# Eight-layer network, top-two experts: tiles stepped by their own age, and one buffer pool opened earlier

## Chip, core and metric

One NeuronCore of a Trainium2 chip runs the whole program in one launch. The metric is device time in microseconds (us); lower is better. Each time is that of one execution, and the median of three executions stands for a kernel.

## The reference

A post-norm stack over x of 4 batch elements, 1024 positions and 128 features: eight sublayers, each followed by `x = layernorm(x + f(x))`. In order: a minGRU, a slot mixer, sparse attention, a two-way routed FFN, a linear "cosformer" attention, a top-two-of-eight expert FFN, a state-space layer (SSM) and a top-p expert FFN. The change is in the sixth, and touches its neighbours, the fifth (called *attention* below) and the seventh (called the *scan*):

```python
def _L2_ffn_ref(x, router_w, w13, w2):          # E, H, I, K = 8, 128, 256, 2
    logits = jnp.einsum('bsh,eh->bse', x, router_w)
    probs = jax.nn.softmax(logits, axis=-1)
    weights, indices = jax.lax.top_k(probs, K)
    weights = weights / (weights.sum(axis=-1, keepdims=True) + 1e-06)
    h13 = jnp.einsum('bsh,ehi->bsei', x, w13)
    gate, up = jnp.split(h13, 2, axis=-1)
    y = jnp.einsum('bsei,eih->bseh', jax.nn.silu(gate) * up, w2)
    y_sel = jnp.take_along_axis(y, indices[..., None], axis=2)
    return (y_sel * weights[..., None]).sum(axis=2)

# of the state-space layer, the step that makes the scan:
h = jnp.exp(d_l[:, :, None] * A) * h + (d_l * x_l)[:, :, None] * b_l[:, None, :]
y_l = jnp.einsum('ben,bn->be', h, c_l)
```

## The kernel before, in words

The program is written with a tile framework. Buffers come from named pools; a pool takes the place of pools closed before it, and what is written into it waits until whatever used that place is done. A planner then orders each engine's instructions by simulated times and priorities; only the TensorE order inside attention is kept as the code writes it (`manual_schedule`). Engines run their queues in order: PE (matmul), DVE (vector), ACT (activation), POOL (GpSimd), and SP, which issues most DMAs.

**Generators as the clock.** Sublayers are Python generators that other loops advance, one `next` at a time. The attention `l2_attn` runs 128 units (4 elements x 4 quarters x 8 head pairs) in steps `t` from -2; each step emits parts of several units and then advances the side generators. In the trace a step takes about 5.9 us.

**Sorting (`l2_dispatch`, one element at a time).** After an element's last attention quarter is normed, its 1024 rows are routed (`router`, L1209 on), counted and placed on DVE with small tiles of the pool `moed` (the variable `md`), and then scattered by 16 indirect DMAs on POOL (L1383) into a DRAM table `xrows` of 23 tiles of 128 rows, sorted by expert. When the scatters are emitted, the element's entry gets `"put"`. For the last element, attention stops its sorting before the scatters and leaves the rest to the scan's loop (`m2["rest"]`).

**Top-two experts (`l2_ffn`, the generator `moe`).** It has 92 units, 4 elements x 23 tiles. A unit goes through five stages: `l2_load_rows` (four tiles of sorted rows, SP, L1442), `l2_weights` (the tile's expert weights, tile `wx`, SP, L1458; 4 buffers), `l2_load_tile` (transposes), `l2_hidden` (eight matmul records into `pa_m` or `ph`, then ACT Tanh L1490 and DVE L1491 and L1494), `l2_expert_out` (four matmul records, ACT copy L1510, and for each fourth tile a store to `yrows`, L1512). In the loop before, one counter `t` places them: rows at unit `t+8`, weights at `t+4`, transposes at `t+2`, hidden at `t`, output at `t-2`. At the top of a step a `while` holds the counter as long as unit `t+8` belongs to an element whose rows have not been put. So when the next element isn't sorted yet, the current element's last tiles are held too: those with weights not yet loaded, not yet hidden, not yet put out. After an element's last tile comes `l2_combine` as a side generator: two halves, each of 8 indirect gathers on POOL (L1529), ACT scaling, DVE adds and a layernorm, some 12 `yield`s a half. It is advanced twice a step, and once a step while the counter is held.

**Who advances `moe`.** In attention, `early` advances it once a step after element 0 has been put and until element 1 is done. When element 0 is done (`st[0]["done"]`), attention also starts `begin`, the preparation of the scan's first half (`l3_prepare`), one part a step. In the scan loop (`l3`), there are 8 halves (element x half of the positions), each of 16 state steps `n`; `moe` is advanced once per `n`, twice in the first half, and `rest` once per `n`.

**The scan (`l3_scan`).** Each `n` loads two rows broadcast over partitions (`bn`, `cn`, SP, L1844), multiplies on POOL (`db`, L1849), takes the exponent on ACT (`da`, L1853), scans on DVE (L1854), multiplies again on POOL (`hc`, L1865), and sums on PE (`pys`). The top-p experts (`l3_ffn`, `ph` and `py`) of finished halves are interleaved, and the last two halves' experts run after the last scan.

**Where the pools lie.** Pools stack from two sides, left and right. On the right, from the end inward: `moek`, `first`, `moet` (the experts' tiles), `w2` (attention's weights: `wE`, `c_turn` and so on), and innermost `moed`. On the left, attention's `cos` is closed when attention ends, and the scan's pools `ssm` (`sq3`, `xc`, `db1` ...) and `ssm2` (`bn`, `cn`, `db`, `hc`, `xnT`, `ud` ...) take its place and more. In the bytes of a partition that the planner gave them: `cos` 59,424 to 126,752, `ssm` 59,424 to 78,144, `ssm2` 78,144 to 156,280, `moed` 150,336 to 159,744 (9,408 long), `w2` 159,744 to 189,504 (29,760 long). `moed` and `w2` are closed together, when attention's code ends; `top` (the top-p experts' tiles) takes their place.

Of the kernel before, what the change touches and what calls it, by code (L numbers as in the profile page):

```python
# [37 lines left out]
NT2 = 2 * T // P + NE - 1  # L38
# [11 lines left out]
def weave(*gens):  # L50

    gens = list(gens)
    while gens:
        for g in gens[:]:
            if next(g, gens) is gens:
                gens.remove(g)


class Net:
# [1342 lines left out]
    def l2_ffn(self, wp):  # L1402

        units = [
            dict(st=st, j=j, n=min(4, NT2 - j // 4 * 4))
            for st in self.m2["st"]
            for j in range(NT2)
        ]  # L1410
        n = len(units)
        side = []
        for t in range(-8, n + 4):
            while t + 8 < n and "put" not in units[max(t + 8, 0)]["st"]:
                for g in side[:]:
                    if next(g, self) is self:
                        side.remove(g)
                yield
            if 0 <= t + 8 < n and units[t + 8]["j"] % 4 == 0:
                self.l2_load_rows(units[t + 8], units, t + 8, wp)  # L1420
            if 0 <= t + 4 < n:
                self.l2_weights(units[t + 4], wp)
            if 0 <= t + 2 < n:
                self.l2_load_tile(units[t + 2], units, t + 2, wp)
            if 0 <= t < n:
                self.l2_hidden(units[t], wp)
            if 0 <= t - 2 < n:
                u = units[t - 2]
                self.l2_expert_out(u, units, t - 2, wp)
                if u["j"] == NT2 - 1:  # L1430
                    side.append(self.l2_combine(u["st"], wp))
            for g in side * 2:
                if next(g, self) is self and g in side:
                    side.remove(g)
            yield
        for g in side:
            yield from g

    def l2_load_rows(self, u, units, i, wp):
        j, n, st = u["j"], u["n"], u["st"]  # L1440
# [720 lines left out]
def program(tc, io):  # L2161
    with ExitStack() as ctx:
        n = Net(ctx, tc, io)
        wd, w0 = ExitStack(), ExitStack()
        wdp = wd.enter_context(tc.tile_pool(name="wd", bufs=1))
        W = n.l0_load(w0.enter_context(tc.tile_pool(name="w0", bufs=1)))
        d = n.l1_ffn_load(wdp)
        dp = ctx.enter_context(
            tc.tile_pool(name="rows", bufs=2, space=bass.MemoryType.DRAM)
        )  # L2170
        sd = ctx.enter_context(tc.tile_pool(name="ssmd", bufs=2, space=bass.MemoryType.DRAM))
        with ExitStack() as ff:
            last = n.front(ff, w0, W, d, dp)
            keep = ctx.enter_context(tc.tile_pool(name="moek", bufs=1, side="right"))
            first = ctx.enter_context(tc.tile_pool(name="first", bufs=1, side="right"))
            mt = ctx.enter_context(tc.tile_pool(name="moet", bufs=2, side="right"))
            w2 = ExitStack()
            n.l2_attn_load(w2.enter_context(tc.tile_pool(name="w2", bufs=1, side="right")))
            weave(*last)
        wd.close()  # L2180
        def load():
            n.l2_ffn_load()
            n.l3_load(sd)
            n.l2_rows(keep, md, dp)

        moe = n.l2_ffn(mt)
        with w2:
            md = w2.enter_context(tc.tile_pool(name="moed", bufs=1, side="right"))
            n.l2_attn(load, n.l2_dispatch, moe, first)
        n.l3_pools(ctx)  # L2190
        fp = ctx.enter_context(tc.tile_pool(name="top", bufs=2, side="right"))
        n.l3(moe, fp)
# [17 lines left out]
```

## Time and profile before

| what | value |
|---|---|
| three executions | 2287.27, 2295.73, 2288.26 us; median 2288.26 |
| the profiled execution | 2286.79 us, of it 2285.0 in the span from first to last instruction |
| mean granted TensorE clock | 0.935 |
| busy: PE, DVE, ACT, POOL | 1978.9, 1349.2, 1210.5, 1023.4 us |
| indirect scatters (L1383) of elements 0 to 3, first to last | 840 to 915, 1007 to 1094, 1216 to 1305, 1371 to 1393 us |
| gathers (L1529) of elements 0 to 3, first to last | 1169 to 1200, 1361 to 1410, 1544 to 1582, 1724 to 1772 us |
| first `db` multiply of the scan's halves 0 to 7 | 1390, 1476, 1563, 1668, 1778, 1871, 1961, 2058 us |

How to read it: times inside the trace count from the start of the span. Attention lies between some 615 and 1340 us, the scan from 1390 to 2147, and from there to 2281 the last experts run on PE. A group row gives an engine, a line, what is written and read, the count, and busy time. A window row gives its length, then the busy time of each engine with its instruction count, the granted clock, and the DMA engines' share. In an answer in order of time, the columns are start, length, engine, line, operation and tiles, and in brackets how long the engine sat idle before it and what is taken to have released it.

### The profile page before, as it was taken

The numbers are of one execution on the slowest core, as the hardware profiler recorded it, in microseconds if no ns is written. First come the engines' busy times: TensorE is split into PE (matmuls) and PEld (weight loads), VectorE is DVE, ScalarE is ACT, GpSimd is POOL, SyncE is SP. The second block draws the span as 40 slices with busy tenths as digits, with TensorE's granted clock in tenths as the row PEclk, the third lists the DMA queues.
The fourth block names the chain that finished last, engine by engine and source line by source line (L and its number), as shares of the span: only waits on it lengthen the run. The fifth ranks groups of instructions, "written<-read, shape, count | busy, mean of one in ns | idle before, by whom it ended". The sixth has DMA issues, their size and how long they took to land.

```text
span 2285.0 us, 46402 instructions
## 1 busy us (share of the span) xinstructions
PE 1978.9 (87%) x17806; PEld 1383.3 (61%) x17806; DVE 1349.2 (59%) x3693; ACT 1210.5 (53%) x2623; POOL 1023.4 (45%) x812
## 2 busy tenths in 40 slices
PE   6667979879999999999989876679899999999998
PEld 3455655444477777787767664246565656565666
DVE  6457843433355565565555555696777688776521
ACT  6543443332244444444455456576768786767443
POOL 5100230000023234224233418998889889879400
PEclk9667989979999999999999988799999999999999
DMA  3000110005000010031223147456786677776421
GB/s 107 0 14 24 30 39 1 19 10 174 1 3 2 3 35 15 17 87 49 65 80 85 37 126 221 135 175 200 216 216 178 174 189 192 193 187 167 119 61 51
DMA packets 138559, 211.10 MB, mean 92 GB/s; under 512 B 18598, under 2 KB 75937, under 8 KB 137953
## 3 DMA queue, kind: packets, MB, share of 16 engines
q1 hardware_dynamic: 126192, 173.87, 25.5%
q0 software_dynamic: 12144, 34.26, 7.1%
q8 instruction: 140, 2.29, 0.4%
q14 instruction: 83, 0.67, 0.1%
HBM read 160.29 MB, written 23.16 MB: 80 GB/s over the span
## 4 chain that ended last, share of the span: by engine, by line
PE 43%; DVE 12%; ACT 11%; issue 3%; DMA 2%; POOL 1%; SPq 0%; ACTq 0%; DVEq 0%; POOLq 0%
PE py L127 7%; PE ph L127 7%; PE po L1126 5%; PE pqk L127 5%; PE pa_m L127 5%; DVE db L1854 4%; PE pys L127 3%; PE kp_mo L127 3%; PE pv L127 2%; PE pr L1196 2%; ACT hh L1980 1%; ACT da L1853 1%; PE pt L131 1%; PE kp_mo L131 1%; ACT xN L174 1%
## 5 line engine op out<-in xcount | busy, mean ns | idle before, releaser
L1059 POOL TENSOR_TENSOR qt<-r_q,sb_c_turn 128x256 f32<-128x256 f32 (+1 forms) x256 | 164.0, 660 | 447.9 <-ACT r_q L1051 442.2
L1865 POOL TENSOR_TENSOR hc<-db,cn 128x1024 f32<-128x1024 f32 x128 | 314.7, 2493 | 57.1 <-PE pys L127 25.6
L127 PEld LDWEIGHTS py<-wh,hh 128*128 128x128 f32 x2048 | 249.8, 192 | 79.9 <-issue 44.8
L1849 POOL TENSOR_TENSOR db<-ud,bn 128x1024 f32<-128x1024 f32 x112 | 286.3, 2633 | 12.4 <-issue 9.9
L127 PE MATMUL ph<-xT,wh 128*128 128x512 f32 x512 | 256.3, 618 | 21.2 <-DVE h_acc L1996 5.8
L127 PE MATMUL py<-wh,hh 128*128 128x128 f32 x2048 | 258.2, 276 | 12.7 <-ACT hh L1980 6.6
L1980 ACT ACTIVATE hh<-ph,sb_cols 128x512 f32<-128x512 f32 x256 | 170.6, 680 | 131.1 <-PE ph L127 104.5
L1117 DVE TENSOR_TENSOR a<-pa_m,sb_c_near 128x256 f32<-128x256 f32 x256 | 96.6, 419 | 203.4 <-PE pa_m L127 203.4
L1074 ACT ACTIVATE kN<-kp_mo,sb_c_trig 128x128 f32<-128x128 f32 x448 | 129.8, 371 | 132.0 <-PE kp_mo L131 122.2
L1853 ACT ACTIVATE da<-dl,aneg 128x512 f32<-128x512 f32 x224 | 153.6, 689 | 74.4 <-DVE db L1854 73.3
L127 PE MATMUL pys<-hc,sb_c_ident 128*128 128x512 f32 x324 | 158.5, 619 | 22.7 <-POOL hc L1865 19.4
L1854 DVE TENSOR_TENSOR_SCAN db<-da,carry,db 128x512 f32<-128x512 f32 x128 | 156.9, 1265 | 11.7 <-ACT da L1853 8.8
L1854 DVE TENSOR_TENSOR_SCAN db<-da,db 128x512 f32<-128x512 f32 x128 | 149.3, 1205 | 10.4 <-POOL db L1849 6.0
L127 PEld LDWEIGHTS ph<-xT,wh 128*128 128x128 f32 x512 | 89.6, 196 | 104.7 <-issue 53.5
L1996 DVE SCALAR_TENSOR_TENSOR h_acc<-py,gt,h_acc 128x128 f32<-128x128 f32 x256 | 71.9, 342 | 125.8 <-PE py L127 125.8
L127 PE MATMUL pqk<-xT,wE 128*128 128x256 f32 x512 | 136.7, 390 | 8.3 <-ACT coT L1193 4.2
L127 PEld LDWEIGHTS pys<-hc,sb_c_ident 128*128 128x128 f32 x324 | 60.5, 199 | 86.7 <-issue 58.7
L729 POOL DMA_INDIRECT orows<-o,ix x20 | 18.9, 944 | 186.0 <-DVE o L727 160.4
L127 PEld LDWEIGHTS pqk<-xT,wE 128*128 128x128 f32 x512 | 88.5, 193 | 21.9 <-DVE cv L1036 8.1
L131 PE MATMUL pt<-sb_c_ident,xN 128*128 128x128 f32 x224 | 54.2, 345 | 51.0 <-ACT xN L174 31.8
L1193 ACT COPY coT<-pt 128x512 f32<-128x512 f32 x64 | 37.5, 586 | 114.9 <-PE pt L131 114.9
L127 PE MATMUL po<-ht,wD 128*128 128x512 f32 x192 | 93.7, 595 | 0.0
(456 smaller groups left out, 4344.1 us busy)
## 6 DMA issues: line engine op xcount, KB each, us to landing
wx<-in_wF SPq DMA_DIRECT2D x92, 384.0 KB, 3.4
bn<-rows SPq DMA_DIRECT2D x128, 256.0 KB, 5.0
cn<-rows SPq DMA_DIRECT2D x128, 256.0 KB, 4.2
wh<-in_wH SPq DMA_DIRECT2D x64, 512.0 KB, 3.8
hc<-hc POOLq DMA_DIRECT2D x47, 512.0 KB, 6.6
xrows<-zero SPq DMA_DIRECT2D x4, 1472.0 KB, 12.3
xg<-xrows SPq DMA_DIRECT2D x20, 256.0 KB, 3.0
yrows<-ys SPq DMA_DIRECT2D x20, 256.0 KB, 3.3
```

The costliest lines, as they stand in the source:

```text
L127: return self.nc.tensor.matmul(out=out, lhsT=lhsT, rhs=rhs, start=start, stop=stop)
L131: self.nc.tensor.transpose(out, in_, self.ident[0:n, 0:n])
L1059: nc.gpsimd.tensor_mul(u["qt"][:, m, a:], u["q"][:, a:], c2["turn"][:, m, o + a : o + 2 * P])
L1074: self.nc.scalar.activation(u["kN"][:, c, m, :], pk[:, c, :], AF.Copy, scale=trig[:, k, m : m + 1])
L1117: nc.vector.tensor_mul(u["a"][:, i, :, :], pa[i], self.c2["near"][:, None, :].to_broadcast([P, 2, P]),)
L1126: self.nc.tensor.matmul(out=u["po"][self.HALF[j], i, c, :], lhsT=lhsT, rhs=rhs, start=key not in u["begun"], stop=True, skip_group_check=True,
L1849: nc.gpsimd.tensor_mul(db, ud, bc[0])
L1853: nc.scalar.activation(da, dl[:, ec, :], AF.Exp, scale=aneg[:, j : j + 1])
L1854: nc.vector.tensor_tensor_scan(db[:, ec, :], da, db[:, ec, :], carry[:, ec, n : n + 1] if h else 0.0, ALU.mult, ALU.add,)
L1865: nc.gpsimd.tensor_mul(hc, db, bc[1])
L1980: nc.scalar.activation(ht, ph, AF.Relu, bias=self.col("h_b1", i=e * NK + k))
L1996: nc.vector.scalar_tensor_tensor(acc[:, c, :], py[:, c, :], gt[:, c, e : e + 1], acc[:, c, :], ALU.mult, ALU.add,)
```

## The change

Two edits. In `l2_ffn` the one counter becomes an age per unit: a unit enters at age 0 when its element's rows are put, one per step, and does rows at age 0, weights at 4, transposes at 6, hidden at 8, output at 10, whether or not another unit follows; the side generators get two advances in every step. In `program` the pool `moed` is opened before `w2` instead of just before attention, so that from the end inward the right side is `moek`, `first`, `moet`, `moed`, `w2`. By the sizes above `moed` then has 180,096 to 189,504 and `w2` 150,336 to 180,096.

```diff
-        n = len(units)
-        side = []
-        for t in range(-8, n + 4):
-            while t + 8 < n and "put" not in units[max(t + 8, 0)]["st"]:
-                for g in side[:]:
-                    if next(g, self) is self:
-                        side.remove(g)
-                yield
-            if 0 <= t + 8 < n and units[t + 8]["j"] % 4 == 0:
-                self.l2_load_rows(units[t + 8], units, t + 8, wp)
-            if 0 <= t + 4 < n:
-                self.l2_weights(units[t + 4], wp)
-            if 0 <= t + 2 < n:
-                self.l2_load_tile(units[t + 2], units, t + 2, wp)
-            if 0 <= t < n:
-                self.l2_hidden(units[t], wp)
-            if 0 <= t - 2 < n:
-                u = units[t - 2]
-                self.l2_expert_out(u, units, t - 2, wp)
-                if u["j"] == NT2 - 1:
-                    side.append(self.l2_combine(u["st"], wp))
+        side, live, k = [], [], 0
+        stages = (
+            (0, lambda i: units[i]["j"] % 4 == 0 and self.l2_load_rows(units[i], units, i, wp)),
+            (4, lambda i: self.l2_weights(units[i], wp)),
+            (6, lambda i: self.l2_load_tile(units[i], units, i, wp)),
+            (8, lambda i: self.l2_hidden(units[i], wp)),
+            (10, lambda i: self.l2_expert_out(units[i], units, i, wp)),
+        )
+        while k < len(units) or live or side:
+            if k < len(units) and "put" in units[k]["st"]:
+                live.append([k, 0])
+                k += 1
+            for at, f in stages:
+                for i, age in live:
+                    if age == at:
+                        f(i)
+            for v in live:
+                v[1] += 1
+            if live and live[0][1] > 10:
+                i = live.pop(0)[0]
+                if units[i]["j"] == NT2 - 1:
+                    side.append(self.l2_combine(units[i]["st"], wp))
             for g in side * 2:
                 if next(g, self) is self and g in side:
                     side.remove(g)
             yield
-        for g in side:
-            yield from g
...
             w2 = ExitStack()
+            md = w2.enter_context(tc.tile_pool(name="moed", bufs=1, side="right"))
             n.l2_attn_load(w2.enter_context(tc.tile_pool(name="w2", bufs=1, side="right")))
...
         with w2:
-            md = w2.enter_context(tc.tile_pool(name="moed", bufs=1, side="right"))
             n.l2_attn(load, n.l2_dispatch, moe, first)
```

## The prediction

> **What bounds the kernel now.** I read the page's slices and chain first, then windows around the place where attention hands over to the scan, then the answers in order of time of each engine there.
>
> ```profile
> PE   6667979879999999999989876679899999999998
> POOL 5100230000023234224233418998889889879400
> PEclk9667989979999999999999988799999999999999
> PE 43%; DVE 12%; ACT 11%; issue 3%; DMA 2%; POOL 1%; SPq 0%; ACTq 0%; DVEq 0%; POOLq 0%
> ```
>
> PE is full in attention (slices 13 to 20) and nearly full from slice 27 to the end; the hole is between, 1200 to 1540 us, where POOL goes from nothing to full. The chain is PE's for long stretches, so a gain must be a hole that closes, not an engine that gets faster. The windows show the hole in columns of length, then PE, PEld, DVE, ACT and POOL busy:
>
> ```profile
> 1265.00:1325.00 60.00, 49.13 (x873) 38.42 (x871) 32.17 (x90) 32.28 (x72) 22.02 (x28) 0.91 0.08 23
> 1325.00:1361.00 36.00, 32.03 (x331) 29.77 (x328) 19.55 (x74) 21.85 (x60) 0.00 (x0) 0.91 0.53 154
> 1361.00:1390.00 29.00, 10.29 (x61) 8.67 (x60) 14.57 (x63) 11.70 (x26) 21.77 (x23) 0.76 0.77 259
> 1390.00:1485.00 95.00, 63.01 (x202) 35.31 (x201) 63.86 (x88) 54.89 (x116) 92.00 (x46) 0.81 0.52 151
> 1485.00:1563.00 78.00, 65.56 (x324) 42.38 (x324) 66.27 (x121) 55.22 (x114) 70.44 (x36) 0.98 0.62 186
> ```
>
> From 1325 to 1361 POOL does nothing; from 1390 to 1485, the scan's first half, it is busy 92.0 of 95 us: POOL is the bound there, and its idle time just before is lost time. Why it idled, in order of time (POOL, then DVE, ACT and SP):
>
> ```profile
> 1323.44 1.41 POOL L1059 TENSOR_TENSOR qt<-r_q,sb_c_turn 128x256 f32<-128x256 f32 x2 [9.59 <-ACT r_q L1051]
> 1361.52 0.99 POOL L1529 DMA_INDIRECT yg<-yrows,di  x1 [36.67 <-DVE ch L1361]
> ...
> 1371.60 0.99 POOL L1383 DMA_INDIRECT xrows<-xN,di  x1 [0.30 <-DVE wt L1377]
> ...
> 1390.31 2.37 POOL L1849 TENSOR_TENSOR db<-xT,bn 128x1024 f32<-128x1024 f32 x1
> ```
>
> ```profile
> 1344.42 1.11 DVE L178 TENSOR_SCALAR xN<-cr,ln_mv,ln_rs 128x128 f32<-128x128 f32 x4
> 1346.29 0.31 ACT L1727 ACTIVATE sq<-xN 128x128 f32<-128x128 f32 x1
> 1371.18 0.24 DVE L1377 TENSOR_TENSOR wt<-wt,sm 128x8 f32<-128x8 f32 x2
> 1371.50 0.33 SPq L1844 DMA_DIRECT2D bn<-rows  x1
> 1371.90 0.67 ACT L1742 ACTIVATE xnT<-pt,sb_cols 128x512 f32<-128x512 f32 x1
> ```
>
> POOL's queue holds element 1's gathers, then element 3's scatters, then the scan's first multiply. The first gather is put down to DVE, but the last store of element 1's tiles to `yrows` was issued at 1357.19, so it waits for those tiles. The scan's inputs wait on their own: `sq`, of pool `ssm`, is written 0.8 us after attention's last norm (1344.42 + 1.11 = 1345.53), when `cos` is done; `bn` and `xnT`, both of `ssm2`, go 0.1 and 0.5 us after the last write of the last sorting (1371.42). `bn` itself lies only where `cos` was; that it waits for sorting says that `ssm2` as a whole waits for `moed`, into which its last 5,944 bytes reach. The first half's own data was ready at about 1324 (its last `ud` write).
>
> **The change, part by part.** *The pool.* With `moed` outside of `w2`, `ssm2` overlaps `cos` and `w2` alone. `w2`'s last reader is the last output matmul (1339.8), `cos`'s the norm at 1345.53, so `bn` can be issued at 1345.5 instead of 1371.5: 26.0 us earlier. With 5.0 us to land (the page's median for `bn`) the first multiply can go at 1350.5 instead of 1390.3, **39.8 us** earlier. It adds no instruction; the place of `moed`'s loads in SP's queue stays. `w2` now waits at its own opening for one closed pool less, at 516 us, 100 us ahead of its first matmul: nothing.
>
> But POOL keeps its other work, and that decides what is left of the 39.8. Gathers and scatters cost 0.96 us plus 0.30 idle, 1.26 each. From 1361.5 POOL did 8 gathers, 16 scatters, 8 gathers (32 x 1.26 = 40.3) and 16 + 16 multiplies at 2.37 and 2.36 (75.7): 116.0, and half 1 began at 1476.3, 114.8 later. So I can schedule it anew. The scatters can't come before sorting ends at 1371; they now come among the multiplies, which have priority in the code, and still cost their 20.2 in that half.
>
> *The ages.* Element 1's rows are put at 1095 and its tiles enter one per step of 5.9 us. The last of the 23 enters 22 steps after the first and is put out at age 10: 32 steps, 1095 + 189 = 1284. Its first 8 gathers follow there and the second 8 six steps on, near 1320, where POOL is busy only 22 of 60 us. Before, these tiles stood still from 1264 to 1325:
>
> ```profile
> 1264.00:1325.00 61.00, 0.13 (x2) 0.00 (x0) 0.92 0.08 24
> 1325.00:1347.00 22.00, 11.12 (x84) 9.90 (x84) 1.00 0.54 158
> 1440.00:1485.00 45.00, 3.69 (x23) 3.70 (x23) 0.77 0.41 122
> ```
>
> (PE and PEld time of `wx` alone; 92 tiles took 161.3 in all, 1.75 each.) So both gather bursts leave the stretch. POOL then has 75.7 + 20.2 = 95.9 to do from 1350.5, and half 1 starts at 1446.4: a lead of **29.9**. With one burst left in it, 19.8; with both, 9.7.
>
> On PE the ages move about 7 tiles, 7 x 1.75 = 12.3 us, from 1325 to 1347 into 1265 to 1325, where PE idled 10.9. The scan's preparation moves forward too: element 0's tail no longer waits, its end comes about ten steps (some 59 us) earlier, and so `begin`. Attention's PE work is the same in sum. Its end could come 10.9 sooner; or it could come later, since the gathers of element 1 now stand in front of `qt` multiplies on POOL, which PE needs: in 1150 to 1200, with element 0's 16 gathers and a sorting, PE idled 50 - 39.5 = 10.5. I take 0, between -10.9 and +10.5.
>
> Element 2's tail held the same way from 1441 to 1485 and ran after; now it runs in the first half, on a PE that idles 32 of 95 us there, and relieves 1485 to 1563, which idled 12.4. That is worth 0 to -12.3; I take 0, because PE has slack on both sides. Its weights are loaded by SP; SP's other work there is `bn` and `cn`, at 0.4 us an issue. Element 0's tail moves from 1097 to 1143 into 1050 to 1097: PE's work trades places, 0.
>
> *Stretched multiplies.* The `db` rows have means of 2372 ns in the first half and 2633 later, when DVE does more. The first half will now run beside the last sorting's DVE work. At worst 32 x 0.26 = 8.4 us, at best 0; I take 2, as that work lasts only from 1351 to 1371. [...]
>
> **Sum.** -29.9 + 2 + 0 + 0 = -28. After half 1 starts nothing waits on an absolute time: the halves, the top-p experts and the 134 us that end the kernel hang on one another, so I let the lead run through. Against the profiled 2286.8 that is 2259; against the median, 1.5 us above that execution, **2260**. The likeliest case's own range: at the slow end POOL keeps both bursts and nothing is stretched, -9.7 (2278), or, for the same sum, both bursts leave, the stretch is the whole 8.4 and attention ends 10.5 later (-11); at the fast end 29.9 with attention 10.9 sooner and half of the 12.3, -47 (2241).
>
> **The rivals.** *The pool isn't what holds `bn`* (some other wait ends with the last sorting). Then `bn` lands at 1376.5 as now, the multiplies go ahead of the scatters, and only the gathers' move counts: from 1376.5 POOL has 95.9, less some 4 scatters already done (5.0), half 1 at 1467: -9, 2279. For it: the release is inferred from two rows. Against: two engines start within 0.5 us of the same event.
>
> *The lead is eaten downstream* (same). From 1485 on PE is busy 84 to 94% of each half, and the first half's experts begin only at 1546, so PE may set the pace; it then starts no earlier than its in-order queue allows. Price: up to the whole 28, 2288. For it: the chain is PE's there. Against: PE's work hangs on the scan's results, and PE idles 18.7 of 29 and 32 of 95 us before.
>
> *SP's queue holds the scan* (slower). A `wx` load waits in SP's queue for one of 4 buffers, that is until an older tile's output is made, and `bn` and `cn` stand behind it. From 1441 to 1485 SP issued no `wx`; now some 8 would stand among that half's loads, at two tiles per `n`. In 1361 to 1485 PE waited 17.1 us in 6 pieces for `wx`, 2.9 on average, the longest 9.9. At the average 8 cost 23 and the result is the same as before; from 3.5 each the change loses; at 5.0, half of the longest, 8 x 5.0 = 40 less 28 is +12: 2300.
>
> **How the numbers follow.** Forecast 0.62, pool not the holder 0.10, lead eaten 0.14, SP's queue 0.14. A change of less than 0.5% (11.4 us) can hardly be told from none here. Faster beyond it (below 2276.8) takes 0.60 of the forecast's case, cut a little at its slow end, and nearly half of the second and a little of the third: 0.68. Slower (above 2299.7) is most of the last: 0.13. The rest, 0.19, is same. The range, 2238 to 2293, takes in the forecast's own 2241 to 2278, the next two cases, and leaves out the worst of the last and the best of all.
>
> **What would show it.** Right: the first `bn` issued near 1346 within 2 us of attention's last norm; the first `db` multiply by 1355, before element 3's scatters; element 1's gathers before 1330; half 1's first `db` near 1447; each later half shifted by as much; PE's clock above 0.81 in the first half. Wrong: `bn` still just behind the last sorting; `wx` loads with `bn` right behind them and POOL waiting on DMA; halves 2 to 7 longer than the 104, 111, 93, 90, 97 and 89 us that they take now; attention's last norm later than 1356.

## The result and the profile after

The changed kernel takes 2325.78 us (median of 4 runs, 2322.17 to 2326.02) against 2290.1 (median of 4) of the kernel before beside it: a ratio of 1.0151, 95% interval 1.0133 to 1.0169. The forecast was 2260, with 2238 to 2293 as its range. The profiled execution took 2326.02 us, its span 2324.2.

The page's slices (busy tenths of PE and POOL, then the granted clock) and its chain:

```profile
PE   6667978979999999999898946669998889899998
POOL 5000220000123244233422367889698969687500
PEclk9767989979999999999999958979999999999999
PE 20%; DVE 10%; ACT 7%; issue 2%; DMA 2%; POOL 1%; SPq 0%; ACTq 0%; POOLq 0%; DVEq 0%
```

POOL now starts a slice earlier (6 in slice 24, where it had 1), but then it is not full for long, and the hole in PE is deeper: 4, 6, 6, 6 from slice 24, with a mean clock of 0.59 in that slice. The parts of the chain come to 42% of the span, where they came to 72%. That is no smaller share of PE: this chain goes back only to 1338 us, to the gathers of element 1, and the earlier one reached back to 622. From there it runs through these gathers and then through DVE's sorting (start, length):

```profile
1342.46 2.52 DMA yg<-yrows,di
1369.34 3.34 DVE rt_p L1238
1388.26 6.97 DVE ch L1361 x2
```

Three stages make the comparison simple: from the start to the scan's first `sq`; from there to the first `gT` (the first half's experts start); from there to the end. The kernel before, in windows (length, busy us and count of PE, PEld, DVE, ACT, POOL, then granted clock, DMA share, GB/s):

```profile
1346.30:1546.70 200.40, 134.62 (x559) 86.15 (x559) 142.10 (x278) 119.75 (x259) 169.69 (x93) 0.85 0.58 175
1546.70:2285.00 738.30, 673.32 (x3421) 446.04 (x3419) 484.81 (x988) 491.94 (x877) 527.61 (x274) 0.98 0.61 164
```

The changed kernel, the same two stages and then the scan's first half alone:

```profile
1354.00:1568.40 214.40, 131.45 (x534) 82.10 (x534) 159.50 (x282) 125.54 (x268) 171.70 (x97) 0.82 0.52 158
1568.40:2324.20 755.80, 682.91 (x3423) 452.28 (x3422) 482.76 (x966) 476.89 (x846) 516.32 (x261) 0.96 0.58 159
1360.90:1477.90 117.00, 71.03 (x325) 47.60 (x325) 91.30 (x157) 58.51 (x137) 86.00 (x47) 0.82 0.56 174
```

The spans of these two executions differ by 39.2 us (the medians of the times by 35.7): 7.7 in the first stage (1346.3 to 1354.0), 14.0 in the second, 17.5 in the third. PE has the same work in the third (3421 and 3423 instructions), and does it at a lower clock (0.96 against 0.98) and with more idle time. In the first half POOL, which was busy 82.9 of 85.9 us before, is busy 86.0 of 117.

The mechanism that the forecast rested on is there. Rows in order of time, DVE, SP's queue and POOL of the changed kernel (its line numbers are one less than before in the scan and in the tiles' stages):

```profile
1351.82 1.12 DVE L178 TENSOR_SCALAR xN<-cr,ln_mv,ln_rs 128x128 f32<-128x128 f32 x4
1353.08 0.33 SPq L1843 DMA_DIRECT2D bn<-rows  x1
1359.92 0.94 POOL L1528 DMA_INDIRECT yg<-yrows,di  x1 [0.30 <-issue]
1360.88 7.03 POOL L1848 TENSOR_TENSOR db<-xT,bn 128x1024 f32<-128x1024 f32 x3
```

The first `bn` goes 0.14 us after attention's last norm (1351.82 + 1.12) and no longer behind the last sorting; the first multiply starts at 1360.88 in place of 1390.31, before element 3's scatters (1415). So 29 us of lead are there at the scan's start, and none of them is left at the first `gT`, which comes 21.7 us later than before.

### The profile page after: what moved, and what is told of

It reads as the page before. It is cut to its first block, busy times and chain, and to the rows that moved or that the text cites. A ratio compares the mean times of both kernels' runs of the same rounds, so it can differ in the third digit from the quotient of the medians.

```text
span 2324.2 us, 46359 instructions
## 1 busy us (share of the span) xinstructions
PE 1984.4 (85%) x17806; PEld 1385.2 (60%) x17806; DVE 1367.9 (59%) x3695; ACT 1201.7 (52%) x2615; POOL 1024.0 (44%) x812
## 5 line engine op out<-in xcount | busy, mean ns | idle before, releaser
L127 PE MATMUL ph<-xT,wh 128*128 128x512 f32 x512 | 258.1, 620 | 23.4 <-ACT hh L1979 11.7
L127 PE MATMUL py<-wh,hh 128*128 128x128 f32 x2048 | 260.1, 279 | 10.5 <-ACT hh L1979 7.3
L1853 DVE TENSOR_TENSOR_SCAN db<-da,carry,db 128x512 f32<-128x512 f32 x128 | 157.1, 1265 | 11.1 <-ACT da L1852 6.5
## 6 DMA issues: line engine op xcount, KB each, us to landing
xrows<-zero SPq DMA_DIRECT2D x4, 1472.0 KB, 11.7
```

The source lines that it names most:

```text
L127: return self.nc.tensor.matmul(out=out, lhsT=lhsT, rhs=rhs, start=start, stop=stop)
L1853: nc.vector.tensor_tensor_scan(db[:, ec, :], da, db[:, ec, :], carry[:, ec, n : n + 1] if h else 0.0, ALU.mult, ALU.add,)
```

## The experiments

All runs by stage. The first column counts from element 0's first scatter, which all kernels reach by the same code, so that what differs earlier drops out. "Half clock" is the time in the last stage that the trace's record of the granted clock has at 0.5; in the traces of before and after the record has only 1.0 and 0.5, in pieces of 3.4 us.

| kernel | scatter to `sq` | `sq` to `gT` | `gT` to end | half clock | ratio to before |
|---|---|---|---|---|---|
| before | 505.8 | 200.4 | 738.3 | 25 | 1 |
| after | 516.5 | 214.4 | 755.8 | 56 | 1.0151 |
| e1 ages alone | 518.0 | 198.7 | 757.8 | 66 | 1.0137 |
| e2 pool alone | 511.6 | 201.3 | 744.7 | 42 | 1.0032 |
| e3 sorting first | 516.5 | 220.8 | 749.4 | 46 | 1.0173 |
| e4 first probe | 509.5 | 205.0 | 734.9 | 26 | one run |
| e5 element 2 held | 516.5 | 201.0 | 739.0 | 46 | 1.0060 |
| e7 late combine | 514.9 | 204.3 | 750.1 | 35 | 1.0098 |
| e9 before, fixed order | 511.5 | 201.5 | 1045.0 | 281 | 1.1348 |
| e10 ages, fixed order | 519.6 | 200.4 | 1027.4 | 250 | 1.1301 |
| f1 before, again | 503.7 | 200.4 | 738.0 | 22 | 0.9993 |
| f2 ages, again | 517.4 | 196.8 | 758.3 | 62 | 1.0100 |
| f3 copies tied | 512.1 | 202.7 | 757.7 | 55 | 1.0088 |
| f4 other order | 508.9 | 200.3 | 749.7 | 36 | 1.0046 |
| f5 second other order | 504.2 | 200.0 | 759.4 | 67 | 1.0076 |
| f6 after, other order | 519.5 | 214.0 | 758.4 | 45 | 1.0186 |
| e8 second probe* | 515.7 | 234.9 | 745.5 | 22 | one run |
| e11 copies tied* | 514.2 | 205.1 | 761.1 | 58 | 1.0028 |
| e12 tied, element 2 held* | 514.3 | 215.8 | 756.1 | 55 | 1.0044 |
| e13 after, fixed order* | 525.8 | 213.2 | 1029.2 | 270 | one run |

The runs with a star were on a chip where the kernel before takes 2332 us (2286 to 2291 on the others); unless the text says otherwise, their stages are compared with each other. Each row of stages is one profiled execution, and the ratio stands for all: e2's profile was 8.3 us above the median of its kernel and e5's 7.9 below it, so a difference of some 8 us in a single cell can be that. In e5, e7, e10, e11, e12, f2 and f3 the pool is back at its old place, as in e1.

### One edit at a time

**e1**, the ages alone (the pool back at its old place):

```
             w2 = ExitStack()
-            md = w2.enter_context(tc.tile_pool(name="moed", bufs=1, side="right"))
...
         with w2:
+            md = w2.enter_context(tc.tile_pool(name="moed", bufs=1, side="right"))
```

> The ages alone: the sorting's pool is opened where it was before, so `bn` waits for the last sorting again. Theory A (the scan's POOL multiplies and the last sorting's DVE instructions hold one another once the pool lets them run side by side): no sorting instruction on DVE longer than 1.2 us after 1361, the first `db` at 1380 to 1395, half 0 at most 100 us, and a time of 2270 to 2300 us. Rival B (the ages cost it: element 2's tail and the later end of attention): the loss stays, 2315 to 2335, with half 0 above 105 us though nothing on DVE is stretched. Rival C (the planner's other order makes halves 4 to 6 late whatever the edit): halves 4 to 6 take 10 us or more longer than the 93, 90 and 97 of before, and the time is 2295 to 2315.

**e2**, the pool alone: `l2_ffn` as it was before, `moed` opened ahead of `w2`.

> The pool alone: the old steps of the tiles, the sorting's pool opened first. Theory A: small sorting instructions (`ch` L1361, `rt_p` L1238, `sel` and their like) take 1.2 to 4.8 us beside the scan's multiplies where they take 0.16 to 0.7 elsewhere, 10 us or more of excess in sum; half 0 takes 110 us or more; the time is 2300 to 2335. Rival B (the ages cost it): half 0 below 100 us, and the time is 2255 to 2290. Rival C: halves 4 to 6 longer by 10 us or more in sum while half 0 may be either; 2295 to 2315.

**e3**, both edits, and the rest of the last sorting with a priority above the scan's (the loop also ends what is left of the scan's preparation and of attention's own side generators, which get that priority too):

```
             for g in (begin, *side):
-                for f in g:
+                with tc.high_priority(offset=4000):
+                    for f in g:
...
```

> Both edits, but the last sorting, which is issued after attention's last norm, is given a higher priority than the scan, so that its DVE instructions are queued ahead of the scan's. Theory A: the sorting ends by about 1380 with at most 4 us of stretched instructions, half 0 takes 95 us or less, and at least 15 us of the 36 us that were lost come back: 2285 to 2310. Rival B: half 0 stays at 105 us or more and the time above 2315. Rival C: half 0 becomes short, but halves 4 to 6 remain 20 us longer in sum than before, and less than 12 us come back: 2312 to 2325.

The ages alone give 2317.94 us, ratio 1.0137 (1.0097 to 1.0178); the pool alone 2292.32, ratio 1.0032 (1.0013 to 1.0050). So theory A in the form in which it was set up falls: no sorting instruction is stretched in e1, and yet most of the loss is there. It was right on e2's first half (119 us, 11.3 us of stretched sorting instructions) and wrong on what that costs. Rival B names the right edit but the wrong place: e1's first half takes 89 us. Its loss lies ahead of the scan and behind the first `gT`, 12 and 19.5 us. e3 is a miss for A: the sorting did not end sooner (its scatters start at 1428, in the changed kernel at 1415), its instructions were stretched by 18.8 us all the same, and the first half took 140 us, as B had it (105 or more). So a place further ahead in the queue did not keep the sorting from the multiplies; why the first half grew by another 23 us isn't shown. Rival C has a part of the place: halves 4 to 6 take 14.7 us more in sum than before with the ages alone, 5.8 with the pool alone and 23.8 with both.

Why the pool alone is worth nothing: its first half in one window.

```profile
1356.00:1474.70 118.70, 76.81 (x291) 50.51 (x290) 86.78 (x164) 66.34 (x150) 101.98 (x63) 0.76 0.61 188
```

POOL has 102 us of work there, and 32 of its instructions are gathers and scatters with 0.30 us of issue each, 9.6 more: it is all but full. The multiplies only went ahead of work that POOL has to do in any case. The first half ends 121.9 us after `sq` (129.9 before), and at the first `gT` even these 8 us are gone (201.3 against 200.4).

### What holds the sorting: POOL's running multiply

In the changed kernel 8 DVE instructions of the last sorting take 18.0 us more than the same forms elsewhere. In order of time, DVE and then POOL:

```profile
1369.26 3.42 DVE L1238 TENSOR_TENSOR rt_p<-rt_l,rt_m 128x64 f32<-128x64 f32 x1
1388.18 7.05 DVE L1361 TENSOR_SCALAR ch<-rt_r 128x64 f32<-128x64 f32 x2
...
1370.26 2.33 POOL L1864 TENSOR_TENSOR hc<-db,cn 128x1024 f32<-128x1024 f32 x1
1390.47 4.71 POOL L1848 TENSOR_TENSOR db<-xT,bn 128x1024 f32<-128x1024 f32 x2
1403.26 2.36 POOL L1864 TENSOR_TENSOR hc<-db,cn 128x1024 f32<-128x1024 f32 x1 [8.07 <-DVE cmp L1318]
```

`rt_p` takes 0.22 us elsewhere; here it ends at 1372.68 with the multiply that ends at 1372.59. The two `ch` (0.19 each elsewhere) end at 1395.2 with the two `db` that end at 1395.18. Seven of the 8 end within 0.1 us of the end of a multiply. The scans queued behind them come late: the two that start at 1400.70 had their `da` at 1387.53 and their `db` at 1388.20. POOL, which waits for the scans, idles in the first half for 26.1 us in six waits ahead of `hc`, the longest 8.07. Not all of that need be the stretch: DVE has 157 instructions in this half, 91.3 us busy, where it had 81 and 57.3, and of the 34.0 us more only 18.0 are stretch. The rest is the sorting itself, which now stands among the scans, and more of the experts' work; no run separates the two causes. Whether it is the running multiply that stretches was measured apart.

**e4** put three small DVE instructions per step of half 0 on tiles of their own into the kernel before:

```
+        for t in src:
+            nc.scalar.copy(t, self.ident[:, 0:64])
+        nc.vector.tensor_single_scalar(out[0], src[0], 2.0, ALU.is_le)
+        nc.vector.reduce_sum(red, src[0].rearrange("p (a b) -> p a b", b=8), AX.X)
+        nc.vector.tensor_add(out[1], src[0], src[1])
```

> The kernel before with 3 extra small DVE instructions per step of half 0, on tiles of their own in SBUF that nothing else reads, beside POOL's multiplies: tensor_single_scalar on 128x64 (one SBUF input, SBUF output), reduce_sum of 128x64 (one SBUF input), tensor_add of two 128x64 (two SBUF inputs), with ACT copies that fill them. If a DVE instruction waits for the POOL instruction that runs (theory A's mechanism), some kinds take up to 2.4 us (one multiply's length) or more, against about 0.2 us alone: I expect tensor_add and tensor_single_scalar to be stretched, with means above 1 us, and reduce_sum to stay below 0.4. If the stretch in the changed kernel came from something else (a semaphore, the order of the queue), all three kinds stay below 0.4 us on average. [...] The extra work should add 5 to 15 us to the time of 2288.

It tells nothing: the planner took the probes ahead, to 1353 to 1379, where POOL does no multiply. All kinds stayed at 0.19 to 0.22 us in the median (0.27 at most), which are the lengths with no multiply beside them. **e8** ties them to the scan by what they read:

```
+            if b == 0 and h == 0:
+                self.probe(da, db)
...
+        nc.vector.tensor_single_scalar(out[0], db[:, 0, 0:64], 2.0, ALU.is_le)
+        nc.vector.reduce_sum(red, db[:, 0, 0:64].rearrange("p (a b) -> p a b", b=8), AX.X)
+        nc.vector.tensor_add(out[1], db[:, 0, 0:64], db[:, 1, 0:64])
+        nc.vector.tensor_single_scalar(out[2], da[:, 0:64], 2.0, ALU.is_le)
```

> The kernel before with four small DVE instructions per step of half 0, placed right behind the scan, so that they run while POOL multiplies: tensor_single_scalar on 128x64 (one input and the output in SBUF), reduce_sum of 128x64 (one SBUF input), tensor_add of two 128x64 (both in SBUF), tensor_single_scalar with its input in PSUM. Alone they take some 0.2 us (0.19, 0.21 and 0.22 in the first probe). If a DVE instruction of some kinds waits for the running POOL instruction, those kinds have means above 0.8 us and single ones above 2 us: I expect the tensor_add and the SBUF to SBUF tensor_single_scalar among them, and not the reduce_sum or the one from PSUM (below 0.3). If the sorting's long instructions had another cause, all four stay below 0.4. [...] With 10 to 60 us of such waiting in half 0, the time would be 2290 to 2340.

The groups of e8 by form (`pb_t` has two inputs in SBUF, `pb_s` one with its output in SBUF, `pb_r` is the reduction, `pb_p` reads PSUM; busy us and mean ns):

```profile
L1887 DVE TENSOR_TENSOR pb_t<-db 128x64 f32<-128x64 f32 x16 | 23.0, 1438 | 0.0
L1885 DVE TENSOR_SCALAR pb_s<-db 128x64 f32<-128x64 f32 x16 | 13.0, 811 | 0.0
L1886 DVE TENSOR_REDUCE pb_r<-db 128x8 f32<-128x64 f32 x16 | 3.3, 207 | 0.0
L1888 DVE TENSOR_SCALAR pb_p<-da 128x64 f32<-128x64 f32 x16 | 3.1, 195 | 0.0
```

Same size, same place, and the kinds part as expected: the additions take 0.21 us at least and 2.39 at most, the SBUF to SBUF scalar instructions up to 4.4 us, nearly two multiplies of 2.35 long, while the reduction and the one from PSUM never exceed 0.22. All 14 that take over 0.5 us end within 0.1 us of the end of a multiply: so the scalar instruction of 2.16 us at 1443.10 and the multiply at 1443.06, the addition of 1.38 us at 1449.50 and the multiply at 1449.42. That is shown, then: in this run a DVE instruction of these two kinds that runs long lasts until POOL's multiply is done. The excess, 23.0 + 13.0 less 32 x 0.2, is 29.6 us, and half 0 took 121 us, where e12 on the same chip took 87 and the kernel before takes 86. The other way round little is seen: of POOL's 31 multiplies in the first half of the changed kernel, one `hc` (at 1383.23) took 2.66 us, the others 2.33 to 2.44.

### Attention's end: copies that wait ahead of attention's own

In the changed kernel, two of POOL's gathers (the first of each burst), then ACT in order of time, then PE:

```profile
1333.66 0.99 POOL L1528 DMA_INDIRECT yg<-yrows,di  x1 [6.04 <-DMA yrows<-ys]
1351.17 0.94 POOL L1528 DMA_INDIRECT yg<-yrows,di  x1 [7.77 <-ACT xN L174]
...
1336.21 0.40 ACT L1545 ACTIVATE yg<-yg,wt 128x128 f32<-128x128 f32 x1 [5.96 <-DMA yg<-yrows,di]
...
1341.82 0.56 ACT L1193 COPY coT<-pt 128x512 f32<-128x512 f32 x1
...
1342.43 2.08 PE L1196 MATMUL pr<-wE,coT 128*128 128x128 f32 x8 [7.47 <-ACT coT L1193]
1346.09 2.08 PE L1196 MATMUL pr<-wE,coT 128*128 128x128 f32 x8 [0.73 <-ACT coT L1193]
```

Element 1's combine now falls at attention's end. Its `yg` copies wait in ACT's queue for the gathers, one by one, and attention's last two `coT` copies stand behind them: the input `pt` of the first was complete at 1334.96 (1334.63 + 0.33), and the copy starts at 1341.82. PE idles 7.47 us, and its clock is at 0.5 from 1336 to 1357 (the group of 8 takes 2.08 us, where the one at 1328.42 took 1.06). Two trials. **e7** starts this combine only when attention is over in the program:

```
+                    if i // NT2 == 1 and "over" not in self.m2:
+                        wait.append(side.pop())
+            if "over" in self.m2:
+                side, wait = side + wait, []
```

> The ages alone, the sorting's pool at its old place, and element 1's combine (its gathers and the ACT copies of `yg` that wait for them) is not started before attention is over. If it is these copies in ACT's queue, ahead of attention's last two `coT` copies, that make attention's end late: PE does not idle 7 us before the last `pr` matmuls, the scan's first `sq` comes at 1344 to 1352 instead of 1359.5, and the time falls by 5 to 13 us from the 2318 of the ages alone, to 2305 to 2313. If the end is late because element 1's tiles take PE's time there: `sq` stays at 1356 or later and the time above 2313.

**e11** (and **f3**, the same kernel, beside which the kernel before and the ages alone were profiled too) ties each of the copies, `q`, behind attention's last norm besides:

```
+                if b == 1:
+                    self.tc.add_manual_dep(q, self.m2["over"].name, SYNC, reason="after attention")
```

> The ages alone, the sorting's pool at its old place, and now the ACT copies of element 1's combine are tied to come after attention's last norm, which the run before only asked for by the place in the program. Measured from element 0's first scatter, the scan's first `sq` came after 506 to 512 us in the runs with the old steps, 517 to 520 with the ages. If the copies in ACT's queue are what makes attention's end late: no idle of 7 us on PE before the last two groups of `pr`, `sq` after 508 to 513 us, and the time 4 to 10 us below the 2318 of the ages alone. If element 1's tiles take the time from attention's own matmuls: `sq` stays at 515 us or more after that scatter.

> The ages with element 1's combine copies tied behind attention's last norm, beside both on the same chip. If these copies are the loss in attention: from the first scatter to `sq` within 4 us of the kernel before, and the time 7 to 13 us below that of the ages alone; the last stage stays longer than before by 8 to 22 us, as nothing is done about it. If not: `sq` as late as with the ages alone, within 4 us.

e7 gives 1.0098 (1.0080 to 1.0116), but `sq` is hardly earlier: the planner took the copies ahead again, and PE still idles 7.10 us there. In f3 they come after:

```profile
1341.82 0.57 ACT L1194 COPY coT<-pt 128x512 f32<-128x512 f32 x1
1342.44 2.08 PE L1197 MATMUL pr<-wE,coT 128*128 128x128 f32 x8 [1.58 <-ACT coT L1194]
```

PE's wait falls from 7.45 us (f2) to 1.58, and `sq` comes after 512.1 us: 5.3 earlier than with the ages alone on that chip (517.4), 8.4 later than the kernel before (503.7). On the other chip the tied copies (514.2) were 1.5 us ahead of the old steps (515.7). f3 meets neither of its expectations (within 4 us of before, or of the ages); f2's 13.7 us lie just past its 7 to 13. The traces part the two costs: from attention's last `r_q` copy (ACT, L1051) to `sq`, the eight profiles with the old steps take 23.1 to 23.9 us, the eight with the ages 28.2 to 28.6, e7 26.8, and the three with tied copies 21.6 to 21.9, on the starred chip as on the others. So the copies cost some 5 us and the tie takes them away. The rest lies ahead of that last `r_q`: 480.3 to 488.4 us from the first scatter with the old steps, 488.0 to 491.2 with the ages (unstarred rows). Time that element 1's tiles take on PE ahead of attention's own matmuls would fit, but no run isolates it, and the kernels with the old steps differ by 8 us there among themselves. And the 5 us aren't seen at the end: f3's ratio is 1.0088 (1.0066 to 1.0110), f2's 1.0100 (1.0083 to 1.0116). On the starred chip the same kernel as f3 has 1.0028 (1.0011 to 1.0045); the ages alone weren't run there.

### The last stage: the same work in another order

**e5** holds element 2's tiles as before, so that the ages act in attention alone:

```
+            if k < len(units) and "put" not in units[k]["st"] and k // NT2 in (3,):
+                for g in side[:]:
+                    if next(g, self) is self:
+                        side.remove(g)
+                yield
+                continue
```

> The sorting's pool at its old place, and the ages for elements 0 and 1 alone: element 2's last tiles stand still for element 3's rows as before. The stages are: start to the scan's first `sq`; from there to the first `gT`; from there to the end. They took 1346, 200 and 738 us before, 1360, 199 and 758 with the ages alone. Theory D (element 1's combine in attention costs the first stage, element 2's early tail costs the last one): first stage stays at 1354 to 1362, the last comes back to 735 to 745, and the time is 2295 to 2308. Theory E (the last stage is longer because the planner puts the same work in another order, whatever element 2 does): the last stage stays at 748 to 762 and the time at 2308 to 2322.

**e9** and **e10** (the kernel before and the ages alone) and **e13** (both edits) take the choice from the planner: PE, ACT and DVE keep the order of the program from half 2 on.

```
+            if i == 2:
+                E = mybir.EngineType
+                c3["ctx"].enter_context(
+                    self.tc.manual_schedule(engines={E.PE, E.Activation, E.DVE})
+                )
```

> The kernel before, with PE, ACT and DVE made to take their instructions in the order of the program from the third half on, where the planner chose before. It is the yardstick for the next run; I expect it slower than 2288, by 0 to 150 us, since the planner overlaps more. What counts is the time from the start of half 2 to the end: 721.6 us before, 728.0 with the ages alone, 744.2 in the changed kernel; and from the first `gT` to the end: 738, 758 and 756.

> The ages alone, with PE, ACT and DVE in the order of the program from the third half on, as in the run just before. Theory E (the planner's order makes the last stage longer): with the same order in both, the time from the first `gT` to the end is within 5 us of that of the kernel before with the same fixed order. Theory D (element 2's early tail leaves something behind that costs the later halves): it stays 12 us or more longer.

> The changed kernel, both edits, with PE, ACT and DVE in the order of the program from the third half on, as in the two runs before with that order (1045.0 us from the first `gT` to the end in the kernel before, 1027.4 with the ages alone). Theory E (the last stage's loss is the planner's order): 1020 to 1035 us from the first `gT` to the end, like the ages alone, though the planner's own order gave 756 against 738. From `sq` to the first `gT`, where the planner still chooses, it keeps the 214 us of the changed kernel (205 to 220) against 200. If the pool opened first leaves something that costs the later halves: above 1040.

e5's last stage is 739.0 us and its time 2304.16, ratio 1.0060 (1.0040 to 1.0079), as theory D had it; its profile lies 7.9 us below that median, so the stage of its median execution may be nearer to 747 (an estimate from these two numbers), between the bands of D and E. But the fixed orders speak against D: in one order for all, the ages do not lengthen the last stage but shorten it by 17.6 us (e9 1045.0, e10 1027.4; e13, on the slower chip, 1029.2, inside the 1020 to 1035 that E gave for it). The 17.6 miss the 5 us of E's forecast for e10, on the other side. So what the edits leave to do behind the first `gT` does not cost more in itself. E's own test is a kernel in which nothing but the order differs. **f4** and **f5** are the kernel before with one line moved:

```
-                    next(end, None)
-                    next(nxt, None)
+                    for g in (end, nxt) if i < 2 else (nxt, end):
+                        next(g, None)
```

```
-                for k in range(4 if n % 8 == 7 else 3):
+                for k in range(4 if n % 8 == (7 if i < 2 else 3) else 3):
```

> The kernel before, profiled on the same chip as the next three, since chips differ (one gave 2332 us for it, the others 2286 to 2291). It sets the stages to compare with: on the first chip 1346 us to the scan's first `sq` (506 after element 0's first scatter), 200 to the first `gT`, 738 from there to the end. The time is that of before, within 0.3%.

> The ages alone once more, beside the kernel before on the same chip. Theory: from the first scatter to `sq` 7 to 13 us longer than before (the combine's copies in ACT's queue), from `sq` to `gT` within 5 us of before, the last stage 10 to 22 us longer, in sum 18 to 35 us (ratio 1.008 to 1.015).

> The kernel before with the same instructions, and one change in the order of the program: from half 2 on, each step advances the next half's preparation ahead of the half that ends, in place of behind it. No work is added or taken, so the planner only comes to another order of the later halves on PE, ACT and DVE. Theory E (the order alone can cost what the ages cost there): the last stage moves by 8 us or more, either way, from that of the kernel before (738 on the first chip). If the order is of little weight and the ages cost the last stage in some other way: it stays within 5 us.

> The kernel before with the same instructions, and a second other order: from half 2 on, the extra step of the experts' work comes after each half's steps 3 and 11 in place of 7 and 15. The first other order cost 11.7 us in the last stage. If the planner's order is of weight in itself, this one moves the last stage from 738 us by 4 us or more, in either direction, and may make the kernel faster; the stages before it stay within 5 us (504 to 512 from the first scatter to `sq`, 200). If the first other order cost only because the preparation went ahead of the half that ends: the last stage stays within 4 us of 738.

**f6** is f4's edit in the changed kernel:

> The changed kernel, both edits, with the first other order (the next half's preparation ahead of the half that ends, from half 2 on). Its last stage took 756 us where the kernel before has 738. If that is the planner's order by accident and not something that the edits leave behind, it can move here by 5 us or more, in either direction; if it is of the edits, it rises about as it did in the kernel before, by 8 to 15 us, or stays within 4. The first two stages are as in the changed kernel: 514 to 519 us from the first scatter to `sq`, 210 to 218 to the first `gT`.

The last stage of f1, then of f5 (the columns as above):

```profile
1545.70:2283.70 738.00, 671.96 (x3421) 446.84 (x3419) 484.67 (x988) 491.87 (x877) 527.60 (x274) 0.99 0.61 165
```

```profile
1544.80:2304.10 759.30, 683.78 (x3421) 456.29 (x3419) 487.14 (x988) 493.09 (x877) 527.41 (x274) 0.96 0.59 160
```

Instruction for instruction the same counts, and 21.3 us more: PE busy 11.8 longer at the lower clock (0.96 against 0.99), idle 9.5 longer. f5's ratio is 1.0076 (1.0057 to 1.0094), f4's 1.0046 (1.0030 to 1.0063), with a last stage of 749.7. So an order alone can cost the last stage what the edits cost it (17.5 and 20). That it was the order that did so in the changed kernel is not shown. f6, 1.0186 (1.0160 to 1.0212), moved its last stage by 2.6 us only, and its expectation had put down "within 4" for a cost that belongs to the edits; another order can come out even by chance, so this is weak, but it does not speak for E. The half clock in the table goes with the order: 22 to 26 us of it with the order of before or nearly that (e4), 35 to 67 with the other orders that the planner came to. In the changed kernel the pieces between 1700 and 2200 lie near the seams between halves (1790, 1814, 1906, 1998, 2101, 2111; the halves begin at 1795, 1898, 1999 and 2099), 37.5 us in sum; in the kernel before it is 17.1 there. The waits of the changed kernel from 1895 to 1912 (us in total, times, longest) show one seam:

```profile
POOL db L1848 <- ACT dl L1813: 13.2, 1, 13.2
PEld pb L127 <- ACT gT L1953: 9.1, 1, 9.1
```

POOL waits 13.2 us for the preparation's last copy `dl`, and PE 9.1 for `gT`, both in ACT's queue.

**e12** puts e11 and e5 together:

> As the run just before, and element 2's tiles stand still for element 3's rows as before, so that the ages act in attention alone and without their combine's copies. If the two costs (attention's end, and the last stage, which went from 758 to 739 us with element 2 held) are separate and are all that the ages cost, they add up: `sq` 508 to 513 us after element 0's first scatter, 735 to 746 us from the first `gT` to the end, and a time of 2285 to 2300, that is within 0.5% of the kernel before. If something else of the ages costs time: above 2302.

Its ratio is 1.0044 (1.0025 to 1.0062), inside the expected band; the stages are not what was expected (514.3 for 508 to 513, and 756.1 for 735 to 746), and without a profile of the kernel before on that chip it isn't known what they should be there. No version that was run is faster than the kernel before.

## Why the prediction was wrong, by its own steps

**The pool: right.** `bn` follows the norm, and `db` starts 29.4 us earlier. It starts 10.4 us later than forecast: the norm ends 7.4 later, and the second burst of gathers still stood in front.

**POOL's new schedule: the step that failed first.** "So both gather bursts leave the stretch. POOL then has 75.7 + 20.2 = 95.9 to do from 1350.5, and half 1 starts at 1446.4: a lead of 29.9." Two things are wrong in it. The gathers come later than worked out: at 1333.7 and 1351.2, not at 1284 and near 1320, and so fall on attention's end. The 32 steps had been taken at 5.9 us, but the trace of before has 32 `r_q` copies, one a step, between 1097 and 1320, which is 7.0 us a step, and so has the trace after. And the sum took what leaves and not what comes: of element 1's 16 gathers 5 stayed behind `sq`, and element 2's 16, of which only 2 came before the first `gT`, all moved in ahead of it (1488 to 1524). POOL has 97 instructions and 171.70 us to do from `sq` to `gT`, where it had 93 and 169.69. Over both halves a lead could come only from POOL's idle time in that stage, 30.7 us before, and that grew to 42.7. With both bursts left in the stretch the step said 9.7, and the pool alone measured 8.0: there the sum holds.

**Stretched multiplies: right in place, wrong in direction and size.** Taken as 2 us (0 to 8.4) on POOL. Measured: 18.0 us on DVE, in 8 instructions, and behind them and the sorting POOL idle in the first half (busy 86.0 of 117 us). From 1360.9 the 95.9 us of POOL's work would have ended at 1456.8; half 1 began at 1477.9. The step asked what DVE's work could cost each POOL multiply (0.26 us at worst) and not what each POOL multiply could cost DVE (2.4). With the old pool the second stage shows none of it (e1 198.7, f2 196.8 against 214.4).

**The ages in attention: 0 taken, between -10.9 and +10.5; measured +10.7** from the first scatter, just past the bad end. The bad end had been put down to gathers ahead of `qt` on POOL; it was ACT's queue in part (5 us), and the ACT copies of a combine that is moved were not counted at all.

**"I let the lead run through": the step that failed most plainly.** The pool alone has 8 us at half 1 and none at `gT`; e5's two first halves took 157 us in place of 173, and its `gT` came no earlier (201.0). The rival "the lead is eaten downstream" describes that; what eats it between half 1 and `gT` no run isolates. No step and no rival held that the last stage could grow by 17.5 us. Why it grew is open: f4 and f5 show that the planner's order alone can cost as much, not that it did here.

The third rival, SP's queue, is not what happened: no multiply of POOL's first half waits for a transfer. PE waited there for `wx`, 11.4 us in 4 pieces, the longest 8.2.

The miss is 66 us, by stages: the first 7.7, the second 42 (28 forecast as a gain, 14 lost), the third 17.5, less 1.2 between the sum (2258.8) and the forecast.

## What to carry to other kernels

When a step moves, count on each engine what leaves a stretch and also what comes into it; a stage whose engine is full to the end gains little from an earlier start. Take the length of a step from the stretch in which the steps lie, not from the mean of the whole. Before two engines are let run side by side, ask in both directions what the longer instruction does to the short ones and to the work that is queued behind them: here DVE instructions of 0.2 us took up to 4.75 beside multiplies of 2.4. And where a planner orders the work, test the weight of the order alone with a neutral edit first: here one moved line costs 11.7 or 21.3 us, as much as the edits under study cost that stage.

## What the hardware showed beyond that

A DVE addition of two 128x64 tiles in SBUF took 0.21 to 0.23 us with no multiply beside it (e4) and up to 2.39 beside POOL's multiplies (e8); a scalar instruction of that size from SBUF to SBUF took 0.14 to 0.27 us and up to 4.41. In the changed kernel the longest of these, a `ch` of 4.75 us, starts at 1390.48 and ends at 1395.23, beside two multiplies that last from 1390.47 to 1395.18.

In the traces of before and after PE's clock is granted as 1.0 or 0.5 in pieces of 3.4 us, and over the runs the last stage's length goes with it: 735 to 738 us with 22 to 26 us of it at half clock, 745 to 759 with 35 to 67 (e5 is the exception, 739 with 46; starred runs and fixed orders left out). From 600 us on, each of the 45 falls in these two traces follows a piece of 3.4 us in which PE was busy for 0 to 69% of it, and each of the 43 returns a piece with 82% or more. No threshold is shown by that: 76 other pieces at 1.0 in which PE was busy for 44 to 69% were followed by 1.0 again. In f5 a reordering cost more than the idle time that came with it: of the 21.3 us that f5 has over f1, 9.5 are idle time and 11.8 are the same number of matmuls taking longer, at a mean clock of 0.96 against 0.99.

One of the chips ran the kernel before at 2332 us, 2% above the others (2286 to 2291), and DVE's instructions had the same lengths there: the scans took 1266 and 1206 ns on average in e8, 1265 and 1205 in before. Why it is slower wasn't tried.
